# Strips of an image by half rows, turned on VectorE instead of TensorE

## The chip, the cores and the metric

The kernel runs on one core of a Trainium2 chip. The metric is the device time of one execution in microseconds (us); of several executions the median is taken. The engines are TensorE (PE, with its weight loads as PEld), VectorE (DVE), ScalarE (ACT), GpSimd (POOL) and SyncE (SP), which only issues DMAs here.

## The reference

The input x is 16 images of 56 x 56 pixels with 384 channels, fp32. Two layers follow one another, each added to its input:

```
x = x + window_attention(group_norm(x))      # 12 heads of 32, windows 7 x 7, image rolled by -3, -3
x = x + depthwise_3x3(group_norm(x))         # signs of the clipped weights
```

The group norm has 32 groups of 12 channels, over all pixels of an image. In the attention, q, k and v are products of the rolled image with a 1152 x 384 matrix; each window of 49 pixels attends to itself with a table of relative positions added, and masks for the windows that the roll has wrapped; a product with a 384 x 384 matrix and a bias follow, and the image is rolled back.

## The kernel before, in words

Channels lie on partitions, in three blocks of 128 (NC = 3). An image is cut into eight strips of seven rolled rows (NS = 8, 392 pixels, ST), numbered s through all images; a strip has two units of four windows (u). The units are the loop: `all_units` goes over 256 of them, and a unit has six slots. In each slot stands heavy work (`heavy`): value and query_key of the next strip, the projection of this one (py), the scores of the next unit. After the heavy work of slot 0 come the sums (L474), the attention products (po, L494), `invert` (ACT L512 and L513, DVE L514 and L515) and `divide` (DVE L522).

Everything else is light work. `at(when, f, ...)` gives it a time in units, and within a unit it is emitted behind the slot whose share of the unit it has reached. So the order of every engine is written out by this plan, and each engine works in that order. Two things are planned so: the second layer of the image before (`plan_conv`: eight taps of DVE for each of 12 bands, L621, and `store`), and the loading of the next image (`plan_load`).

Loading a strip before the change: `fetch` issues DMAs on SP's queue that bring whole pixels, 1536 bytes each, into one of two staging tiles (xl, pixels on partitions). `load` then, for each block c, has PE turn four pieces of 112 pixels into a PSUM bank (pl, L322), ACT copy the 392 columns into the strip's tile x in the order of windows (L325), and DVE take the statistics (bn_stats, L329). When the last strip is there, `norm_gather` and `norm_scale` make the image's coefficients by a chain of small DMAs and POOL operations. The first image's strips are loaded ahead of the loop in the same way. PSUM has four banks for pl, pq, pv, po, py and px in turn (`bank`), and the scores have the other four (ps). POOL's queue also has the copy and store of each strip's result (L553, L556) between the layers. The attention result `ot` comes from the pool `two`.

The last strip of an image wraps: it has four rows from the bottom and three from the top.

Of the kernel before, what the change touches and what calls it, by code (L numbers as in the profile page):

```python
# [9 lines left out]
F32 = mybir.dt.float32  # L10
# [5 lines left out]
WIN = 7  # L16
SHIFT = WIN // 2
# [17 lines left out]
def kernel(  # L35
# [12 lines left out]
    nc = tc.nc  # L48
    P = 128
    B, H, W, C = x.shape  # L50
    NH = rel_table.shape[1]
    D = C // NH
    NC = C // P
    HPC = P // D
    T = WIN * WIN
    NS = H // WIN
    NW = W // WIN
    ST = WIN * W
    UW = 4
    UPS = NW // UW  # L60
    NU = NS * UPS
# [2 lines left out]
    NB = H // BR  # L64
    R = W + SHIFT
    LT = 2 * W
    NL = -(-ST // LT)
    QT = HT + T
    OT = 2 * W
# [7 lines left out]
    const = ctx.enter_context(tc.tile_pool(name="const", bufs=1))  # L77
    dram = ctx.enter_context(tc.tile_pool(name="dram", bufs=3, space=bass.MemoryType.DRAM))
    xpool = ctx.enter_context(tc.tile_pool(name="x", bufs=11))
    io = ctx.enter_context(tc.tile_pool(name="io", bufs=3))  # L80
    two = ctx.enter_context(tc.tile_pool(name="two", bufs=2))
    vpool = ctx.enter_context(tc.tile_pool(name="v", bufs=2))
    ptpool = ctx.enter_context(tc.tile_pool(name="pt", bufs=3))
    bpool = ctx.enter_context(tc.tile_pool(name="xb", bufs=2))
# [2 lines left out]
    small = ctx.enter_context(tc.tile_pool(name="small", bufs=2))  # L87
# [3 lines left out]
    def bank(name):  # L91
        return ps.tile([P, 512], F32, tag="mm", name=name)
# [21 lines left out]
    vq = const.tile([P, 4, NW // 2, NC, D], F32, tag="vq", name="vq")  # L114

    xls = [const.tile([P, NL, C], F32, tag=f"xl{n}", name=f"xl{n}") for n in range(2)]

    es = const.tile([P, NH, 2, HT], F32, tag="e", name="e")

# [7 lines left out]
    def clear():  # L127
        for xl in xls:
            nc.gpsimd.memset(xl[:, NL - 1, :], 0.0)

        for t in spare:
            nc.gpsimd.memset(t[:, NL - 1, :], 0.0)

    def clear_more():
        nc.gpsimd.memset(power, -0.5)
        nc.gpsimd.memset(ones, 1.0)
        nc.gpsimd.memset(least, LEAST)
        nc.gpsimd.memset(seen, 0.0)
        for t in (qk[:, :, ST:], *hps):
            nc.gpsimd.memset(t, 0.0)  # L140

    def clear_again():
        for t in spare:
            nc.vector.memset(t, 0.0)
# [87 lines left out]
    stats, coefs, parts = {}, {}, {}  # L232
# [16 lines left out]
    def norm_scale(key, queue, pool=nc.gpsimd):  # L249

        gt = parts.pop(key)
        name = "%d_%d" % key
        g = small.tile([GROUPS, 4], F32, tag="g", name=f"g{name}")
        mean, var, rstd, shift = (g[:, n : n + 1] for n in range(4))
        if key[0]:
            var = seen[:GROUPS, key[1] : key[1] + 1]
        dev = small.tile([GROUPS, GS], F32, tag="dev", name=f"dev{name}")

        def fold(x):

            n = GS
            while n > 1:
                half = n // 2
                pool.tensor_tensor(x[:, :half], x[:, :half], x[:, n - half : n], ALU.add)
                n -= half

        pool.tensor_copy(dev, gt[:, :, 0])
        fold(dev)
        pool.tensor_scalar(mean, dev[:, 0:1], 1.0 / GS, None, ALU.mult)
        pool.tensor_tensor(dev, gt[:, :, 0], mean.to_broadcast([GROUPS, GS]), ALU.subtract)  # L270
        pool.tensor_tensor(dev, dev, dev, ALU.mult)
        pool.tensor_tensor(dev, dev, gt[:, :, 1], ALU.add)
        fold(dev)
        pool.tensor_scalar(var, dev[:, 0:1], 1.0 / GS, EPS, ALU.mult, ALU.add)
        nc.gpsimd.tensor_tensor(rstd, var, power[:GROUPS], ALU.pow)
        pool.tensor_tensor(shift, mean, rstd, ALU.mult)
        pool.tensor_scalar(shift, shift, -1.0, None, ALU.mult)
        both = small.tile([GROUPS, GS, 2], F32, tag="both", name=f"both{name}")
        pool.tensor_copy(both, g[:, 2:4].unsqueeze(1).to_broadcast([GROUPS, GS, 2]))
        by_channel = dram.tile([C, 2], F32, tag="cod", name=f"cod{name}")  # L280
        queue.dma_start(by_channel.rearrange("(g n) k -> g (n k)", n=GS), both.rearrange("g n k -> g (n k)"))
        coef = small.tile([P, NC, 2], F32, tag="coef", name=f"coef{name}", bufs=4)
        queue.dma_start(coef, by_channel.rearrange("(c p) k -> p c k", p=P))
        coefs[key] = coef
# [4 lines left out]
    xs = {}  # L289

    def staging(s):

        if NS > s >= 2 and s < 2 + len(spare) and staged:
            return spare[s - 2]
        return xls[s % 2]

    def fetch(s):
        b, r = divmod(s, NS)
        xl = staging(s)
        first = r * WIN + SHIFT  # L300
        for odd in range(2):
            t, end = 0, (WIN + 1 - odd) // 2
            while t < end:
                row = (first + odd + 2 * t) % H
                n = min(end - t, (H - row + 1) // 2)
                rows = x[b, row : row + 2 * n - 1 : 2].rearrange("t w c -> w t c")
                here = xl[odd * W : (odd + 1) * W, t : t + n, :]
                for lo, hi in ((SHIFT, SHIFT + 48), (SHIFT + 48, W), (W, R)):
                    nc.sync.dma_start(here[lo - SHIFT : hi - SHIFT], rows[lo % W : (hi - 1) % W + 1])
                t += n  # L310

    def load(s, c):
        b, r = divmod(s, NS)
        if (0, b) not in stats:
            stats[0, b] = small.tile([P, NC, NS, 6], F32, tag="st0", name=f"st0_{b}", bufs=1)
        if c == 0:
            xs[s] = xpool.tile([P, NC, ST], F32, tag="x", name=f"x_{s}")
        pt = bank(f"pl_{s}_{c}")
        for t in range(NL):

            n = min(LT, max(ST - t * LT, HT + 1))
            nc.tensor.transpose(  # L322
                pt[:, t * LT : t * LT + n], staging(s)[:n, t, c * P : (c + 1) * P], ident[:n, :n]
            )
        nc.scalar.copy(  # L325
            xs[s][:, c, :].rearrange("p (w r c) -> p r w c", r=WIN, c=WIN),
            pt[:, :ST].rearrange("p (r w c) -> p r w c", w=NW, c=WIN),
        )
        nc.vector.bn_stats(stats[0, b][:, c, r, :], xs[s][:, c, :])  # L329


# [310 lines left out]
    def at(when, f, *args):  # L642
        side.setdefault(int(when), []).append((when, f, args))
# [20 lines left out]
    def plan_load(b):  # L664

        for r in range(NS):
            when = NU * (b - 1) + max(1.3 + 1.2 * r, 2 * r - 3.9)
            if r < 2:

                at(max(NU * (b - 1) - 3 + 1.5 * r, 0.1 * r), fetch, b * NS + r)  # L670
            for c in range(NC):
                at(when + 0.9 * c / NC, load, b * NS + r, c)
            if r + 2 < NS:
                at(when + 0.7, fetch, b * NS + r + 2)
        at(when + 0.8, norm_gather, (0, b), nc.gpsimd)
        at(when + 0.9, norm_scale, (0, b), nc.gpsimd)

# [78 lines left out]
    with tc.manual_schedule():  # L756
        nc.scalar.preload_act_table_set("natural_log_exp_and_others")
        clear()
        staged.append(None)
        for s in range(2 + len(spare)):  # L760
            fetch(s)
        staged.clear()
        fetch_weights()
        clear_more()
        load_bias(nc.gpsimd, 0, 38, True)
        for s in range(NS):
            for c in range(NC):
                load(s, c)
            if s + 2 + len(spare) < NS:
                fetch(s + 2 + len(spare))  # L770
            if s % 2 and s > 1:
                load_weights(s // 2 - 1)
        norm_gather((0, 0), nc.sync)
        clear_again()
        norm_scale((0, 0), nc.sync, nc.vector)
        load_bias(nc.gpsimd, 38, T, True)
        load_weights(NC)
        load_depthwise()
        add_bias(True)
        normalize(0)  # L780
        all_units(True)


        worst = small.tile([P, 2], F32, tag="worst", name="worst")
        for n in range(2):
            nc.vector.tensor_scalar(reach[:, n], reach[:, n], MOST[n], None, ALU.is_lt)
        nc.vector.tensor_reduce(worst[:, 0:1], reach.rearrange("p n u -> p (n u)"), AX.X, ALU.min)
        fine = small.tile([P, B], F32, tag="fine", name="fine")
        nc.vector.tensor_scalar(fine, seen, 1.0e37, None, ALU.is_lt)
        nc.vector.tensor_reduce(worst[:, 1:2], fine, AX.X, ALU.min)  # L790
        pf = bank("pf")
        nc.tensor.matmul(pf[:, 0:2], ones, worst, start=True, stop=True)
        both = small.tile([P, 1], F32, tag="both_fine", name="both_fine")
        nc.vector.tensor_reduce(both, pf[:, 0:2], AX.X, ALU.add)
        nc.vector.tensor_scalar(again, both, -1.0, 2.0 * P, ALU.mult, ALU.add)
# [65 lines left out]
```

## Time and profile before

| | us |
|---|---|
| median of 3 runs (4452.28 to 4455.99) | 4454.59 |
| profiled execution, own time | 4451.33 |
| its span | 4449.5 |
| PE busy | 4267.8 (96%) |
| DVE busy | 3300.8 (74%) |
| ACT busy | 2372.4 (53%) |
| POOL busy | 488.8 (11%) |
| strip transposes, PE L322 (1488 from xl) | 199.1 |
| ACT copy out of PSUM, L325 | 198.9 |

In the profile's rows, "busy, mean ns" are the time of a group of like instructions and of one of them; behind the second bar stands the idle time of the engine ahead of them and what ended it. Busy times of PE overlap, because matmuls are pipelined: four transposes that show 0.56 us delay what follows by less. The 1.8 us between the span and the execution's own time lie around the span. In an answer by stretches, each row gives the length and the busy time of each engine within it; in an answer on waits, each row gives who waited for whom, the total, the number of times and the longest.

### The profile page before, as it was taken

Reading aid. Unit: us, or ns where it says so; the run is one execution under the profiler, and the core shown is the slowest. Engines: PE = TensorE matmul, PEld = TensorE weight load, DVE = VectorE, ACT = ScalarE, POOL = GpSimd, SP = SyncE. Lnnn points to the kernel's source line nnn. Section 1 sums busy time; section 2 is a strip of 40 time slices with the busy share of each in tenths; the row PEclk is TensorE's granted clock in tenths of the full one; section 3 lists DMA queues with packets and bytes.
Section 4 is the critical chain, followed back from the end, with each engine's and each line's share of the span. In section 5 each row is a group of like instructions: output and inputs, shape, how many; then the busy total and the mean of one; then the engine's idle time right before and its main releaser. Section 6 shows DMA issues by size and latency. Waiting matters only on the chain.

```text
span 4449.5 us, 156099 instructions
## 1 busy us (share of the span) xinstructions
PE 4267.8 (96%) x69481; PEld 2759.0 (62%) x69481; DVE 3300.8 (74%) x4267; ACT 2372.4 (53%) x4549; POOL 488.8 (11%) x1200
## 2 busy tenths in 40 slices
PE   5999999999999999999999999999999999999961
PEld 3666666666666666666666666666666666666641
DVE  3445777777777777777777777777777777777878
ACT  2445555555555555555555555555555555555542
POOL 3001110111102011010111101011110101111000
PEclk8999999999999999999999999999999999999985
DMA  3323444444444444344444444444444444433332
GB/s 89 72 64 84 96 99 117 96 103 105 103 94 109 109 94 112 91 99 115 93 107 108 99 96 106 111 97 105 99 102 107 96 110 103 108 94 86 95 89 88
DMA packets 987323, 439.24 MB, mean 99 GB/s; under 512 B 843490, under 2 KB 945387, under 8 KB 986642
## 3 DMA queue, kind: packets, MB, share of 16 engines
q1 hardware_dynamic: 960000, 344.92, 36.2%
q0 software_dynamic: 24464, 81.86, 5.2%
q8 instruction: 550, 9.01, 0.9%
q10 hardware_dynamic: 2178, 2.38, 0.2%
q14 instruction: 131, 1.07, 0.1%
HBM read 169.69 MB, written 158.47 MB: 74 GB/s over the span
## 4 chain that ended last, share of the span: by engine, by line
PE 94%; DVE 3%; DMA 1%; issue 1%; ACT 0%; SPq 0%; POOL 0%; ACTq 0%; DVEq 0%; POOLq 0%
PE pq L349 35%; PE pv L362 17%; PE py L533 17%; PE ps L403 7%; PE po L494 7%; PE ps L474 4%; PE pl L322 3%; PE px L632 3%; DVE o L621 2%; DMA xl<-in_x_dram 0%; SPq L385 0%; DMA out_dram<-xo 0%; DMA mvd<-mv 0%; DMA e<-in_x_dram 0%; DMA vq<-in_x_dram 0%
## 5 line engine op out<-in xcount | busy, mean ns | idle before, releaser
L349 PE MATMUL pq<-xn,wq_t 128*128 128x392 f32 x4608 | 1616.4, 498 | 2.2 <-issue 1.2
L621 DVE SCALAR_TENSOR_TENSOR o<-hp,dw_t,o 128x784 f32<-128x784 f32 x1536 | 1560.9, 1021 | 31.9 <-ACT o L608 17.7
L349 PEld LDWEIGHTS pq<-xn,wq_t 128*128 128x128 f32 x4608 | 837.1, 189 | 551.9 <-issue 6.6
L356 ACT COPY qk<-pq 128x392 f32<-128x392 f32 x768 | 373.3, 486 | 859.0 <-PE pq L349 858.3
L533 PE MATMUL py<-ot,wo_t 128*128 128x392 f32 x2304 | 819.7, 498 | 4.0 <-DVE ot L522 4.0
L362 PE MATMUL pv<-xn,wq_t 128*128 128x392 f32 x2304 | 821.1, 497 | 1.2 <-ACT xn L338 1.2
L514 DVE SCALAR_TENSOR_TENSOR ln<-ps,inv 128x588 f32<-128x588 f32 x256 | 197.3, 771 | 750.1 <-ACT inv L513 729.1
L533 PEld LDWEIGHTS py<-ot,wo_t 128*128 128x128 f32 x2304 | 420.3, 190 | 268.2 <-DVE ot L522 4.1
L362 PEld LDWEIGHTS pv<-xn,wq_t 128*128 128x128 f32 x2304 | 417.0, 189 | 270.8 <-ACT xn L338 2.4
L369 ACT COPY vt<-pv 128x392 f32<-128x392 f32 x384 | 190.1, 495 | 553.3 <-PE pv L362 553.2
L403 PEld LDWEIGHTS ps<-qk 32*64 32x64 f32 x24576 | 307.9, 131 | 149.2 <-issue 103.8
L438 ACT ACTIVATE e<-e 128x1176 f32<-128x1176 f32 x256 | 302.8, 1183 | 176.8 <-DVE e L420 176.8
L420 DVE SCALAR_TENSOR_TENSOR e<-ps,bias 128x1176 f32<-128x1176 f32 x256 | 350.2, 1368 | 38.8 <-PE ps L403 33.5
L494 PE MATMUL po<-e,v 49*32 49x49 f32 x24576 | 363.9, 212 | 12.4 <-DMA v<-vq 7.7
L494 PEld LDWEIGHTS po<-e,v 49*32 49x32 f32 x24576 | 355.4, 105 | 17.7 <-issue 13.4
L553 POOL COPY y<-y 128x63 f32<-128x63 f32 x128 | 32.1, 251 | 2915.8 <-DVE y L541 2915.8
L403 PE MATMUL ps<-qk 32*64 32x49 f32 x24576 | 341.6, 225 | 5.0 <-issue 4.5
L329 DVE BATCH_NORM_STATS2 st<-x 128x6 f32<-128x392 f32 x384 | 214.8, 561 | 135.1 <-ACT x L325 133.9
L632 PE MATMUL px<-ident,o 128*112 128x128 f32 x1344 | 202.6, 286 | 103.2 <-DVE o L621 89.2
L541 DVE TENSOR_TENSOR y<-py,x 128x392 f32<-128x392 f32 x384 | 215.8, 562 | 98.1 <-PE py L533 92.4
L325 ACT COPY x<-pl 128x392 f32<-128x392 f32 x384 | 198.9, 520 | 167.8 <-PE pl L322 167.8
L373 DVE STREAM_TRANSPOSE vq<-vt 128x512 f32<-128x512 f32 x384 | 269.0, 702 | 6.0 <-ACT vt L369 5.8
(114 smaller groups left out, 3486.5 us busy)
## 6 DMA issues: line engine op xcount, KB each, us to landing
v<-vq SPq DMA_DIRECT2D x2048, 48.0 KB
mid<-y POOLq DMA_DIRECT2D x112, 619.5 KB
out_dram<-xo SPq DMA_DIRECT2D x192, 336.0 KB
xb<-mid SPq DMA_DIRECT2D x96, 472.0 KB
xb<-mid SPq DMA_DIRECT2D x96, 442.5 KB
xl<-in_x_dram SPq DMA_DIRECT2D x108, 288.0 KB
xl<-in_x_dram SPq DMA_DIRECT2D x108, 216.0 KB
out_dram<-xo SPq DMA_DIRECT2D x64, 168.0 KB
```

What stands on the lines that cost most here:

```text
L349: nc.tensor.matmul(pq[:, :ST].rearrange("p (w t) -> p w t", t=T), wq_t[:, c, m * P : (m + 1) * P], xn[:, c, :, :T], start=(c == 0), stop=( ...
L356: nc.scalar.copy(qk[:, m, :ST], pq[:, :ST])
L362: nc.tensor.matmul(pv[:, :ST].rearrange("p (w t) -> p w t", t=T), wq_t[:, c, 2 * C + m * P : 2 * C + (m + 1) * P], xn[:, c, :, :T], start= ...
L373: nc.vector.transpose(vq[:, :, :, m].rearrange("p h n d -> p n h d"), vt[:, m].rearrange("p (n w) (j b) -> p n (w j) b", w=2, b=D),)
L403: nc.tensor.matmul(pp[row * HT : (row + 1) * HT, i, k0 : k0 + T], qk[part, NC * fast + j, q0 : q0 + HT], qk[part, NC * (not fast) + j, q0 ...
L420: nc.vector.scalar_tensor_tensor(e, pp[:, :, : NC * 2 * T].rearrange("q i (n k) -> q i n k", k=T), QSCALE, bias[:, int(s % NS == NS - 1)]. ...
L438: nc.scalar.activation(flat, flat, AF.Exp, accum_out=reach[:, 0, u : u + 1])
L494: nc.tensor.matmul(po[w][i * D : (i + 1) * D, (2 * j + r) * T : (2 * j + r + 1) * T], vs[s][keys, n * 2 + r, h * D : (h + 1) * D], by_head ...
L533: nc.tensor.matmul(py[:, :ST], wo_t[:, c, m * P : (m + 1) * P], ots[s][:, c, :], start=(c == 0), stop=(c == NC - 1),)
L541: nc.vector.tensor_tensor(view.rearrange("p r (w c) -> p w r c", c=WIN), py[:, :ST].rearrange("p (w r c) -> p w r c", r=WIN, c=WIN), xs[s] ...
L621: nc.vector.scalar_tensor_tensor(acc, hp[:, dy : dy + BR, dx : dx + W], dw_t[:, c, t : t + 1], acc, ALU.mult, ALU.add)
L632: nc.tensor.transpose(po[:OT, c * P : (c + 1) * P], flat[c][:, t * OT : (t + 1) * OT], ident)
```

## The change

Strips of the images 1 to 15 are brought in another form. `fetch_halves` takes one channel block of a strip and issues, on POOL's queue, one DMA for each 32 of its channels (four a block, 12 a strip; four times as many for the last strip of an image, which wraps). Each brings 15 half rows of 28 pixels; pixel t of a half row goes to partition t of the quarter, and a piece is 32 channels of one pixel, 128 bytes. Once all of a strip is there, `turn_halves` turns the whole tile in squares of 32 by one VectorE instruction, from xl into a new tile xt, so that channels lie on partitions. `arrange` then has ACT copy xt into the strip's tile x in the order of windows: two copies for the two halves of the rows, and a small one for the last three columns, which the roll takes from the other end; DVE's bn_stats follows as before. Nothing of the first image's loading changes, and `load` stays for it. The pool `two` has one buffer where it had two, which makes room for xt, and POOL clears both staging tiles between the first image's last strip and the loop.

```diff
-    two = ctx.enter_context(tc.tile_pool(name="two", bufs=2))
+    two = ctx.enter_context(tc.tile_pool(name="two", bufs=1))
...
+    xt = const.tile([P, NC, NR, D], F32, tag="xt", name="xt")
...
+    def halves(s):
+        flat = xls[s % 2].rearrange("p t c -> p (t c)")[:, : NC * NR * D]
+        return flat.rearrange("p (c k d) -> p c k d", c=NC, d=D)
+
+    def fetch_halves(s, c):
+        b, r = divmod(s, NS)
+        xz = halves(s)
+        flat = x[b].rearrange("h w c -> (h w) c")
+        first = r * WIN + SHIFT
+        rows = min(WIN, H - first)
+        cut = HR - SHIFT
+        for i in range(HPC):
+            def move(k, n, token, lo=0, hi=HR):
+                nc.gpsimd.dma_start(
+                    xz[i * D + lo : i * D + hi, c, k : k + n, :],
+                    flat[token : token + n * (hi - lo)].rearrange("(k t) c -> t k c", k=n)[
+                        :, :, c * P + i * D : c * P + (i + 1) * D
+                    ],
+                )
+            start = first * W + SHIFT - HR
+            if rows == WIN:
+                move(0, NR, start)
+                continue
+            n = 2 * rows
+            move(0, n, start)
+            move(n, 1, start + n * HR, 0, cut)
+            move(n, 1, 0, cut, HR)
+            move(n + 1, NR - n - 1, SHIFT)
+
+    def turn_halves(s):
+        nc.vector.transpose(
+            xt.rearrange("p c k d -> p (c k d)"), halves(s).rearrange("p c k d -> p (c k d)")
+        )
+
+    def arrange(s, c):
...
+        to = xs[s][:, c].rearrange("p (h w r c) -> p h r w c", h=2, r=WIN, c=WIN)
+        for h in range(2):
+            nc.scalar.copy(
+                to[:, h], xt[:, c, 1 + h : 1 + h + 2 * WIN - h : 2, :HR].rearrange("p r (w c) -> p r w c", c=WIN)
+            )
+        nc.scalar.copy(to[:, 1, :, NW // 2 - 1, WIN - SHIFT :], xt[:, c, 0 : 2 * WIN : 2, HR - SHIFT : HR])
         nc.vector.bn_stats(stats[0, b][:, c, r, :], xs[s][:, c, :])
...
             when = NU * (b - 1) + max(1.3 + 1.2 * r, 2 * r - 3.9)
+            s = b * NS + r
             if r < 2:
-                at(max(NU * (b - 1) - 3 + 1.5 * r, 0.1 * r), fetch, b * NS + r)
+                for c in range(NC):
+                    at(max(NU * (b - 1) - 3 + 1.5 * r + 0.3 * c, 0.1 * r), fetch_halves, s, c)
+            at(when, turn_halves, s)
             for c in range(NC):
-                at(when + 0.9 * c / NC, load, b * NS + r, c)
-            if r + 2 < NS:
-                at(when + 0.7, fetch, b * NS + r + 2)
+                at(when + 0.2 + 0.2 * c, arrange, s, c)
+                if r + 2 < NS:
+                    at(when + 0.7 + 0.3 * c, fetch_halves, s + 2, c)
...
         clear_again()
+        for xl in xls:
+            nc.gpsimd.memset(xl, 0.0)
```

HR is 28 (half a row), NR is 15, D is 32 and HPC is 4.

More of the change, by code (lines that the diff above doesn't have):

```diff
@@ L66 @@
     LT = 2 * W
+    HR = W // 2
+    NR = 2 * WIN + 1
     NL = -(-ST // LT)
@@ L328, in load @@
         )
+        nc.vector.bn_stats(stats[0, b][:, c, r, :], xs[s][:, c, :])
+    def halves(s):
[30 more added lines that the diff above has]
+    def arrange(s, c):
+        b, r = divmod(s, NS)
+        if (0, b) not in stats:
+            stats[0, b] = small.tile([P, NC, NS, 6], F32, tag="st0", name=f"st0_{b}", bufs=1)
+        if c == 0:
+            xs[s] = xpool.tile([P, NC, ST], F32, tag="x", name=f"x_{s}")
+        to = xs[s][:, c].rearrange("p (h w r c) -> p h r w c", h=2, r=WIN, c=WIN)
[4 more added lines that the diff above has]
+        nc.scalar.copy(to[:, 1, :, NW // 2 - 1, WIN - SHIFT :], xt[:, c, 0 : 2 * WIN : 2, HR - SHIFT : HR])
         nc.vector.bn_stats(stats[0, b][:, c, r, :], xs[s][:, c, :])
```

## The prediction

> **What bounds the kernel now.** I read the page's first two parts, then the chain that ended last, then the stretches of one image, then the order of time around single strips.
>
> ```profile
> PE 4267.8 (96%) x69481; PEld 2759.0 (62%) x69481; DVE 3300.8 (74%) x4267; ACT 2372.4 (53%) x4549; POOL 488.8 (11%) x1200
> ...
> PE   5999999999999999999999999999999999999961
> PEclk8999999999999999999999999999999999999985
> ```
>
> PE is busy 9 tenths or more from the second slice to the 38th, at the full clock. The chain, asked for 340 to 3941 us, is PE alone; the strips' transposes (pl, L322) hold 3.7% of it:
>
> ```profile
> by line: PE pq L349 36.7%; PE pv L362 18.3%; PE py L533 18.2%; PE ps L403 7.7%; PE po L494 7.3%; PE ps L474 4.0%; PE pl L322 3.7%; PE px L632 3.5%; issue 0.3%; DMA out_dram<-xo 0.1%; ACT xn L338 0.1%; ACT xo L633 0.0%; ACT e L438 0.0%; ACT
> ```
>
> One image is 16 units. Cut at the unit starts of the eighth image (columns: stretch, length, busy PE, PEld, DVE, ACT, POOL, clock, DMA share), units 1 to 10 hold all eight strip loads of the next image, 11 to 15 none:
>
> ```profile
> 1959.79:2127.37 167.58, 167.58 (x2740) 109.05 (x2739) 130.27 (x171) 93.97 (x182) 13.71 (x36) 1.00 0.45 104
> 2127.37:2208.12 80.75, 80.75 (x1340) 51.69 (x1340) 60.77 (x74) 45.33 (x86) 12.12 (x30) 1.00 0.47 107
> ```
>
> PE has no idle there; DVE has 37.3 us of 167.6, and the waits say where it goes:
>
> ```profile
> DVE ln L514 <- ACT inv L513: 26.8, 10, 5.2
> DVE st L329 <- ACT x L325: 5.9, 5, 2.0
> ```
>
> Once a unit DVE stands waiting for ACT's reciprocal (2.7 us on average): it has caught up with PE. That wait is DVE's reserve.
>
> **What the Trainium skill says.** "VectorE: DVE Perf Modes", section The three transpose paths: VectorE turns only blocks of 32 by 32, each for itself. The trace has this instruction (L373, row below). "DMA: Bandwidth & Descriptors", section Specifications: under 512 bytes a piece a transfer is below line rate. The trace agrees: q1's 786,432 packets of 128 bytes (SBUF to SBUF) take 13.3 ns each, 9.6 bytes a ns; its packets of 1536 bytes 96 ns, 15.9 bytes a ns. The same page, section SWDGE vs HWDGE vs iDMA: a DMA issued from GpSimd has its descriptors computed in software there, gathered into packets of preferably at most 4096 bytes. The trace agrees on the gathering: a coef load of 384 pieces of 8 bytes shows as 16 packets. "SBUF — State Buffer", section Who interferes with whom: a VectorE instruction with two SBUF inputs contends with GpSimd instructions that read SBUF. The trace shows nothing of it for DMA issues: L621 takes 1015 ns beside a POOL DMA issue (167 cases), 1021 ns with POOL idle.
>
> **Part 1: transposes leave PE.** 15 images x 8 strips x 3 channel blocks = 360 groups of four. What a group costs is not its busy time but how far it pushes the next matmul:
>
> ```profile
> 2111.57 1.27 PE L494 MATMUL po<-e,v 49*32 49x49 f32 x96
> 2112.77 0.56 PE L322 MATMUL pl<-ident,xl 112*128 112x112 f32 x4
> 2113.17 0.55 PE L362 MATMUL pv<-xn,wq_t 128*128 128x392 f32 x1
> ...
> 2127.90 1.26 PE L494 MATMUL po<-e,v 49*32 49x49 f32 x96
> 2129.09 0.60 PE L349 MATMUL pq<-xn,wq_t 128*128 128x392 f32 x1
> ```
>
> With a group: 2112.77 to 2113.17, 0.40 us. Without one, the next matmul starts where the group did (1.19 us after po against 1.20). Counted over the trace, 150 groups behind po or ps cost 0.404 us and 210 behind large matmuls 0.350: 60.6 + 73.5 = **134 us off PE**. (3.7% of the chain would make 145; I take the start-to-start sum.) They also leave 360 uses of the four PSUM banks, a relief I count as nothing.
>
> **Part 2: DVE gets a turn a strip.**
>
> ```profile
> L373 DVE STREAM_TRANSPOSE vq<-vt 128x512 f32<-128x512 f32 x384 | 269.0, 702 | 6.0 <-ACT vt L369 5.8 <-issue 0.2
> L513 ACT ACTIVATE inv<-ln 128x588 f32<-128x588 f32 x256 | 177.5, 693 | 8.1
> L438 ACT ACTIVATE e<-e 128x1176 f32<-128x1176 f32 x256 | 302.8, 1183 | 176.8 <-DVE e L420 176.8
> L325 ACT COPY x<-pl 128x392 f32<-128x392 f32 x384 | 198.9, 520 | 167.8 <-PE pl L322 167.8
> ```
>
> The turn moves 3 x 15 x 32 = 1440 elements a partition. In proportion to L373 that is 1.97 us; with L373's time as one element a cycle of 0.96 GHz (533 ns) plus 169 fixed it is 1.67. I take 1.67, x120 = **200 us of DVE**. It waits for 12 landings or more, whose waits I put at 0.25 us (bounds 0 and 0.5; a wait instruction on DVE shows 21 ns). In units 1 to 10: 130.3 + 8 x 1.92 = 145.6 us in 167.6 - 24 x 0.373 = 158.6 us, 92%. Idle left: 13 us, where L514 and st now wait 32.7. It fits only if DVE runs 1.9 us a unit later behind PE.
>
> **Part 3: ACT.** One copy of 392 out of PSUM (520 ns) becomes two of 196 and one of 21 out of SBUF. From L513 and L438: (1183 - 693)/588 = 0.83 ns an element, 203 fixed. So 2 x 366 + 220 = 0.95 us, +0.43 a block, **+156 us**, 58% of the shorter span; if these patterns cost twice the slope, +270. Beside PE's work. New waits: ACT waits for the turn, and queued behind it are the qk and vt copies that free PSUM banks for PE and feed the scores. The arrange is put at least one of a unit's six slots (2.8 us) behind the turn, so ACT waits only where DVE is over 1.1 us late. Then bn_stats waits for ACT as it does now, 0.43 us longer.
>
> **Part 4: the loads go from SP to POOL.** Some six SP issues a strip become 12 POOL DMAs (48 for an image's last strip): 132 an image. The nearest row, 384 pieces each:
>
> ```profile
> L283 POOL DMA_DIRECT2D coef<-cod x30: 800/802/807, 288.5 to 4087.1; - x30
> ```
>
> At 0.8 us, about 100 us an image, 37% of POOL's time, against 11% now. A strip takes 9.6 us to issue where strips follow at 1.2 units (19 us). Behind it on POOL: the norm chains (units 0 and 10.9 of an image, no fetch between -0.9 and 2.0 or after 8.6), the y copies and mid stores, delayed by at most four issues, 3.2 us, whose readers come units later. Landing: that coef load has landed 2.4 us after its issue begins. One fetch is 420 pieces of 128 bytes; at 13 ns and 30 pieces an engine 0.4 us of DMA. The last quarter is issued 1.1 units (17 us) before its turn. A strip adds 12 x 0.4 x 14/16 = 4.2 us an engine where the old pieces took 392 x 96/16 = 2.4 us; in these units the DMA share goes from 0.45 to about 0.55. Price 0; bounds: the HBM read of 128 bytes isn't in the trace; at three times 13 ns it still fits (12.6 of 19 us). SP's relief: 0 to 3 us.
>
> **Part 5: ot with one buffer, the clearing.** The ACT copy into ot follows matmuls that stand behind the last readers (py) in PE's order; price 0. The two memsets on POOL (1536 elements each; a memset of 928 takes 0.86 us on POOL, so 2.9 for both) fall in POOL's 21 us wait for DVE's variance; price 0, at most 2.9.
>
> **What comes late next.** In odd units, PE's py waits for DVE's division (L522), which ends 0.8 to 2.1 us ahead of it on average over the images. Five of eight strips lose one or two PE groups just there, 0.35 to 0.75 us, while ACT, which sets L514's start, has 0.43 us a block more and sometimes waits for a turn. The exponential ends 2.7 to 4.7 us ahead of its readers. So a lag of 1.9 us is mostly but not wholly carried. I let a fifth of the turn through, 0.34 us a strip x 120 = 41 us. Bounds: 0; and 0.67 us, 80.
>
> **Sum.** Against the profiled execution: 4451.3 - 134 + 41 = 4358. The median of the runs is 3.3 us above it: **4361 us**.
>
> **Rivals.** *All is hidden:* 4454.6 - 134 = 4320. For it: L514's 2.7 us waits. Against: the 0.8 us ahead of py. *DVE becomes the bound in units 1 to 10 (slower):* turn, its waits and the three longer arranges pass to PE in full, 1.92 + 1.3 = 3.2 us a strip, less 1.12 saved, x 120 = +250: 4705. It decides from 1.12 us of stall a strip on, that is if two thirds of a turn get through. For it: 92% and in-order waits; against: DVE catches up each unit, and in units 11 to 15 has 25% left. *The pieces land late:* the point is 1.6 us a DMA (19/12). At 2 us, 8 x 24 - 159 = 33 us an image, +500. Against: 0.8 to issue, 2.4 to land. *Nothing moves:* stalls match 134 us. That transposes stay is excluded: the plan calls load no more for images 1 to 15.
>
> **How the numbers follow.** 0.2% (9 us) is about what a measurement tells from no change. All hidden or nearly (under 4335) 0.22; partly hidden, to 4400, 0.48; to 4440, 0.15: faster 0.85. Within 9 us: 0.03. DVE bound 0.08 and late pieces 0.04: slower 0.12. The range 4316 to 4440 leaves some 0.03 below and 0.15 above.
>
> **What would show it.** L322 at 96 matmuls, PE near 4135 us busy; a turn at 1.6 to 2.0 us; L514's wait halved; PE waits for DVE ot (py) or ACT of some tens of us; POOL near 48%. It is wrong if DVE waits for x's landing in most turns, if POOL's issue exceeds 1.5 us, or if PE idles over 134 us in the middle.

## The result, and the profile after

The changed kernel takes 4298.76 us (median of 4, 4297.24 to 4300.28) against 4455.29 for the one before: ratio 0.9649, 95% interval 0.9632 to 0.9666, 156.5 us less. The forecast was 4361, range 4316 to 4440: right in direction, and too slow by 62 us. The profiled executions differ by 152.6 us (4451.33 and 4298.77); the traces below account for these.

First the engines' row of the page after, then the chain for 330 to 3800 us:

```profile
PE 4125.1 (96%) x68041; PEld 2628.4 (61%) x68041; DVE 3478.0 (81%) x4387; ACT 2479.2 (58%) x5269; POOL 1800.4 (42%) x3182
```

```profile
by line: PE pq L404 38.2%; PE pv L417 19.0%; PE py L588 18.8%; PE ps L458 7.9%; PE po L549 7.5%; PE ps L529 4.1%; PE px L687 3.7%; issue 0.1%; DMA xb<-mid 0.1%; DVE e L475 0.1%; DMA out_dram<-xo 0.1%; DVE o L676 0.1%; DVE xt L368 0.0%; ACT 
```

The chain is PE as before, without pl; the turn (xt) holds 0.0% of it, and no strip load shows. The same stretches of the eighth image, units 1 to 10 and 11 to 15 (length, then busy PE, PEld, DVE, ACT, POOL, clock, DMA share, GB/s):

```profile
1886.22:2044.77 158.55, 158.55 (x2650) 100.60 (x2658) 140.02 (x175) 101.21 (x230) 84.44 (x144) 1.00 0.50 110
2044.77:2125.52 80.75, 80.75 (x1347) 51.60 (x1355) 62.76 (x79) 45.29 (x86) 29.65 (x55) 1.00 0.52 111
```

Units 1 to 10 went from 167.58 to 158.55 us, where the forecast's sum without stalls had 158.6. DVE is at 88%, and PE still has no idle time. Units 11 to 15 have not changed. The new instructions, and DVE's wait for their data:

```profile
L368 DVE STREAM_TRANSPOSE xt<-xl 128x1440 f32<-128x1440 f32 x120 | 200.4, 1670 | 0.4 <-DMA xl<-in_x_dram 0.4
L380 ACT COPY x<-xt 128x196 f32<-128x196 f32 x720 | 225.8, 369 | 93.8 <-DVE xt L368 92.6
L383 ACT COPY x<-xt 128x21 f32<-128x21 f32 x360 | 76.5, 212 | 11.4
L351 POOL DMA_DIRECT2D xl<-in_x_dram x1980 | 1328.8, 724 | 179.7 <-DVE xt L368 105.1 <-issue 29.0 <-DMA mid<-y 24.9
```

A turn takes 1.67 us; of 120 turns one waited for a load, 0.4 us. And DVE's reserve over the whole execution, before, after, and after in units 1 to 10 of the eighth image:

```profile
DVE ln L514 <- ACT inv L513: 729.1, 247, 8.4
```

```profile
DVE ln L569 <- ACT inv L568: 536.5, 236, 8.4
```

```profile
DVE ln L569 <- ACT inv L568: 14.6, 9, 2.6
```

It is 193 us less, but not all of that went to the 200 us of turns: the units are shorter too, and the run without the turn below parts the two. In units 1 to 10 of the second to the fifteenth image this wait fell from 2.7 us to 1.5 on average, and in 15 of these 140 units nothing was left of it.

### The profile page after: what moved, and what is told of

The parts are those of the page before. It is cut to its first block, busy times and chain, and to the rows that moved or that the text cites. A ratio compares the mean times of both kernels' runs of the same rounds, so it can differ in the third digit from the quotient of the medians.

```text
span 4297.0 us, 155602 instructions
## 1 busy us (share of the span) xinstructions
PE 4125.1 (96%) x68041; PEld 2628.4 (61%) x68041; DVE 3478.0 (81%) x4387; ACT 2479.2 (58%) x5269; POOL 1800.4 (42%) x3182
## 4 chain that ended last, share of the span: by engine, by line
PE 94%; DVE 3%; DMA 1%; issue 1%; ACT 0%; SPq 0%; POOL 0%; ACTq 0%; DVEq 0%; POOLq 0%
PE pq L404 36%; PE pv L417 18%; PE py L588 18%; PE ps L458 7%; PE po L549 7%; PE ps L529 4%; PE px L687 3%; DVE o L676 2%; SPq L440 0%; DMA xl<-in_x_dram 0%; DMA wl<-in_L_conv_w_out_dram 0%; DMA xn<-in_x_dram 0%; DMA out_dram<-xo 0%; DMA vq<-in_x_dram 0%; DMA e<-in_x_dram 0%
## 5 line engine op out<-in xcount | busy, mean ns | idle before, releaser
L404 PE MATMUL pq<-xn,wq_t 128*128 128x392 f32 x4608 | 1591.4, 497 | 0.0
L351 POOL DMA_DIRECT2D xl<-in_x_dram x1980 | 1328.8, 724 | 179.7 <-DVE xt L368 105.1
L569 DVE SCALAR_TENSOR_TENSOR ln<-ps,inv 128x588 f32<-128x588 f32 x256 | 197.0, 769 | 540.2 <-ACT inv L568 536.5
L380 ACT COPY x<-xt 128x196 f32<-128x196 f32 x720 | 225.8, 369 | 93.8 <-DVE xt L368 92.6
L688 ACT COPY xo<-px 112x384 f32<-112x384 f32 x448 | 195.1, 482 | 123.7 <-PE px L687 94.1
```

The source lines that it names most:

```text
L351: nc.gpsimd.dma_start(xz[i * D + lo : i * D + hi, c, k : k + n, :], flat[token : token + n * (hi - lo)].rearrange("(k t) c -> t k c", k=n) ...
L404: nc.tensor.matmul(pq[:, :ST].rearrange("p (w t) -> p w t", t=T), wq_t[:, c, m * P : (m + 1) * P], xn[:, c, :, :T], start=(c == 0), stop=( ...
```

## The experiments

Twelve kernels ran, each beside the kernel before on the same chip (medians 4451.9, 4452.6 and 4454.5 us in the three batches). The kernel after was not run again in them, so a difference to its 4298.76 us can be off by the some 3 us by which these medians differ.

**The price of PE's groups.** On the kernel after, in `plan_load`:

```diff
             for c in range(NC):
+                at(when + 0.9 * c / NC, groups, s, c)   # bank(), then four transposes of ident
                 at(when + 0.2 + 0.2 * c, arrange, s, c)
```

> The kernel after, with the 360 groups of four transposes put back on PE at their old times, of a constant (the identity) into a PSUM bank that nobody reads; loads, turn and arrange stay as changed. Theory A (a group costs 0.35 to 0.40 us on PE, 138 us in all with the slower second matmul behind it, and the rest of the 156 us came from somewhere else than PE's own work): 4437 us, 138 above the kernel after. Theory B (all 156 us are the groups' own price, 0.43 us each): 4455 us, back at the kernel before.

Measured: 4430.35 us, ratio to before 0.9955 (0.9941 to 0.9968). The groups cost 131.6 us by the medians, or 136 by the two ratios to before: as theory A has it, and within 3 us of the forecast's count. But with all of PE's old work back, the kernel is still 21.6 us faster than the one before. Theory B falls. In the traces, 224 units from the second image on (from the first attention product of a unit to that of the next) take 3711.0 us before and 3693.5 here, with the same number of matmuls.

Where these 17.5 us were, PE's waits of the kernel before tell (340 to 4218 us; total, times, longest):

```profile
PE po L494 <- issue: 4.0, 3, 1.6
PE ps L403 <- issue: 3.5, 9, 0.6
PE pq L349 <- issue: 1.2, 2, 0.8
```

"issue" means that PE waited for nothing the profile shows. One of them, in unit 11 of the seventh image, in order of time:

```profile
1860.11 1.22 PE L494 MATMUL po<-e,v 49*32 49x49 f32 x91
1862.88 0.32 PE L494 MATMUL po<-e,v 49*32 49x49 f32 x5 [1.55 <-issue]
```

PE stops in the midst of 96 matmuls whose inputs all lie there, and takes up the last five after 1.55 us of idle time. In the trace's instruction queue (q8, 550 packets of 16 KB for the 140,266 instructions that PE has in the trace, so some 256 in a packet) a packet begins 0.14 us ahead of the stop, counted from the start of the last matmul ahead of it, and ends 1.92 us after it, 2.06 us long where the median is 1.1. Of the ten packets that begin within 4.5 us behind the store of unit 11 (below), nine last 1.7 to 3.1 us. For the stops in the scores the sign is another one: the packets beside those of the list last 0.9 to 1.4 us, but all ten of over 0.25 us from start to start fall on the same place of PE's instructions counted modulo 256 (193 or 194), wherever in its unit that place lies. So the traces are read here as PE running out of instructions: 96 small matmuls and their loads are used up in 1.3 us, and the next packet was late. The longest stop is followed by six matmuls at down to half speed, 1.7 us more together.

**What makes the packets late.** Five edits of the kernel before. Without the strips' DMAs:

```diff
-                at(max(NU * (b - 1) - 3 + 1.5 * r, 0.1 * r), fetch, b * NS + r)
+                pass
...
-            if r + 2 < NS:
-                at(when + 0.7, fetch, b * NS + r + 2)
```

> The kernel before, without the strips' DMAs of images 1 to 15 (their strips are left as they lie in the staging tiles, so x of these images is not loaded; everything else runs). Theory A (the strips' DMAs on SP's queue held up PE's instruction supply: some 18 stalls without a releaser, 13 to 15 us, in units 2, 8 and 11 of an image): 4441 us, the stalls gone. Theory B (the stalls belong to PE's own instruction stream and are not due to these DMAs): 4455 us, the stalls still there.

Measured: 4441.56, ratio 0.9977 (0.9969 to 0.9985), 10.4 us less. PE's waits in the same stretch:

```profile
PE po L494 <- issue: 6.7, 7, 1.5
PE pq L349 <- issue: 0.6, 1, 0.6
```

The stops in the scores, which were in units 2, 4 and 8, are gone from the list; those of unit 11, in the attention and just behind it, stay. Theory A is half right.

In unit 11 it is the next image's norm that begins: POOL stores the statistics to DRAM (mvd, 384 pieces of 8 bytes), 0.8 us ahead of the unit. Planned later:

```diff
-        at(when + 0.8, norm_gather, (0, b), nc.gpsimd)
-        at(when + 0.9, norm_scale, (0, b), nc.gpsimd)
+        at(when + 0.95, norm_gather, (0, b), nc.gpsimd)
+        at(when + 1.0, norm_scale, (0, b), nc.gpsimd)
```

> The kernel before, with the norm of the next image (norm_gather and norm_scale of the strips) planned 0.15 and 0.1 units later, in unit 11 behind the attention instead of at the end of unit 10. Theory A (in the kernel before, the small store of the statistics, issued 0.8 us ahead of unit 11, slows the fetch of PE's next block of instructions just when the attention's short matmuls use it up): the stalls in unit 11 go, some 8 us faster than the kernel before. Theory B (these stalls are due to the place in PE's instruction stream alone): no change, the stalls stay in unit 11.

Measured: 4445.58, 0.9987 (0.9979 to 0.9995), 7 us less. The stops in the attention are gone, but stops in unit 11 are not: they moved from 1.55 to 9.6 us into it, 3.6 us behind the store's new place (5.93), where the next scores are. They follow the store, not a place in the program. The same with the strips' DMAs gone:

> The kernel before, without the strips' DMAs of images 1 to 15 (their strips are not loaded, as in the run without strip DMAs) and with the norm planned later. Theory A (two disturbances of PE's instruction supply add up): all stalls without a releaser go, 18 to 20 us off the kernel before, 4432 us, the time of the changed kernel with its groups put back. Theory B: as the run without strip DMAs, 4441 us.

Measured: 4439.89, 0.997 (0.9959 to 0.9981), not the 4432 of theory A, since the later store only hits other matmuls: unit 11 keeps 4.9 us in its trace (table below). So the store was left out instead:

```diff
+        if key[0] == 0 and key[1] > 0:
+            by_channel = first_channels[0]     # image 0's
+        else:
...
             by_channel = dram.tile([C, 2], F32, ...)
             queue.dma_start(by_channel.rearrange("(c p) k -> p c k", p=P), mv)
...
```

> The kernel before, without the store of the first statistics of images 1 to 15 to DRAM (their coefficients are made from image 0's). Theory A: the stalls of unit 11 go, those of units 2 and 8 stay, 8 to 10 us below the kernel before. Rival: no change.

Measured: 4439.80, 0.9966 (0.9952 to 0.9979), 14.7 us less, more than the 8 to 10 expected. What stays are the scores alone:

```profile
PE ps L410 <- issue: 3.7, 8, 0.8
```

> The kernel before, without the strips' DMAs of images 1 to 15 and without the store of these images' first statistics to DRAM (the coefficients of the first layer are made from image 0's; strips are not loaded). Theory A (PE's instruction supply is disturbed by two things, the strips' DMAs and the small store ahead of unit 11): all stalls without a releaser go, 4432 us, some 20 us below the kernel before, the time of the changed kernel with its groups put back. Rival (the store isn't it): 4441 us, as without the strips' DMAs alone, stalls still in unit 11.

Measured: 4433.87, 0.9953 (0.994 to 0.9967), 20.7 us less. In its list of PE's waits for that stretch there is no line at all, as in that of the kernel with the groups put back. Theory A, in its second form, holds: two disturbances, 10 and 15 us by themselves, 21 together, where the intervals are 4 to 6 us wide to each side. The time of all 224 units in the traces shows which disturbance sits where, in us above this run, by the unit of the image:

| kernel before | unit 2 | 8 | 14 | 11 | all |
|---|---|---|---|---|---|
| as it is | 3.9 | 2.0 | 3.1 | 8.9 | 17.8 |
| no strips' DMAs | 0.1 | 0.1 | -0.2 | 11.2 | 11.9 |
| store later | 3.6 | 0.9 | 2.9 | 4.4 | 14.4 |
| no strips' DMAs, store later | 0.0 | 0.3 | -0.3 | 4.9 | 5.5 |
| no store | 4.7 | 1.1 | 3.0 | 0.1 | 9.4 |

The strips' DMAs cost in units 2, 8 and 14, the store in unit 11. Each row is one execution; that without strips' DMAs was its kernel's second slowest of 14, so its sum is above what the medians say. A rival would be the PSUM banks: in the run with the groups put back, no copy of ACT holds the banks of pl any more. The traces answer it: this run has all the old copies out of these banks, and its 224 units take 3693.2 us, against 3693.5 there.

In the kernel after one line is left (340 to 4070 us):

```profile
PE ps L458 <- issue: 0.8, 2, 0.5
```

The strips no longer come by SP. Their gathered packets from POOL hardly stopped PE here, but they are no proof against it: in the trace of the kernel after without its turn (next part), the slowest of five executions, three stops, 3.5 us together, stand in the scores of unit 4, at the same place modulo 256 (193).

```profile
PE ps L458 <- issue: 3.5, 3, 1.5
```

The store is issued 1.46 us into unit 11 and not 0.8 us ahead of it, as the attention's burst ends. With the groups put back it is issued 0.36 us into it, and without the turn at its start; neither trace has a stop in unit 11. So in all three kernels, whose strips come by POOL, a store 0.8 to 2.2 us later than before goes with no stop in unit 11. That this shift is the cause was not tried by moving the store back alone.

**What the turn costs.** On the kernel after, without the turn:

```diff
-            at(when, turn_halves, s)
...
+        nc.vector.memset(xt, 1.0)
```

> The kernel after without any turn (the tile that the turn writes is filled once, so the strips of images 1 to 15 hold a constant; loads, arranges and everything else run, but nothing on the engines waits for the loads). Theory A (the turn and its wait for the loads cost nothing on the path): within 5 us of the kernel after. The forecast's term: some 20 to 40 us faster than the kernel after.

Measured: 4297.34 (0.9656, 0.9643 to 0.9669), 1.4 us below the kernel after by the medians and 3 above it by the ratios: the turn costs nothing that can be told from zero. What it uses up on DVE shows beside the kernel after, first without the turn, then with it:

```profile
DVE ln L569 <- ACT inv L568: 624.4, 253, 8.4
DVE st L384 <- ACT x L383: 120.4, 92, 3.4
```

```profile
DVE st L384 <- ACT x L383: 41.8, 45, 2.1
```

88 us of the turns' 200 come out of the wait for the reciprocal (624.4 to 536.5) and 79 out of the statistics' wait for ACT. The other 105 us that the reserve lost against before (729.1 to 624.4) are not the turn's. With a second one right behind it (the call to `nc.vector.transpose` twice):

> The kernel after, with each strip's turn issued twice in a row (the second repeats the first): DVE has 1.67 us a strip more, 200 us in all. Theory A (DVE's wait for ACT's reciprocal, 536 us in the kernel after, is a reserve that takes up added DVE work): within 10 us of the kernel after, that wait down to some 380 us. The forecast's term (a fifth of a turn gets through to PE): 40 us or more slower than the kernel after.

Measured: 4337.78 (0.9748, 0.9734 to 0.9761), 39 us slower. That is the forecast's fifth, but for the second turn, not the first. DVE's reserve fell as theory A said, yet PE waits now:

```profile
DVE ln L572 <- ACT inv L571: 412.1, 172, 8.4
ACT x L383 <- DVE xt L371: 263.4, 101, 4.3
PE pv L420 <- DVE y L599: 22.4, 27, 1.2
PEld pv L420 <- ACT e L496: 22.5, 13, 1.8
```

412 us of reserve are left and are of no use, for they lie elsewhere: in units 1 to 10 0.66 us a unit are left, and none in 69 of 140 units. ACT stands up to 4.3 us for the turns, with the copies that PE needs behind it. The same second turn, half a unit away:

```diff
             at(when, turn_halves, s)
+            at(when + 0.65, turn_halves, s)
```

> The kernel after, with a second turn of each strip that stands half a unit behind the first (behind the three arranges) instead of back to back. DVE's total is that of the run with the turn twice. If DVE's total load sets the cost: 4338 us as there. If it is the length of one block of DVE work ahead of the copies and sums that wait for it: within 15 us of the kernel after, 4315 us or less.

Measured: 4303.82 (0.9661, 0.9648 to 0.9674), 5 us slower than the kernel after, with the same DVE work as the run before:

```profile
DVE ln L569 <- ACT inv L568: 403.3, 145, 8.4
ACT x L380 <- DVE xt L368: 126.7, 86, 3.6
```

The reserve is as low (0.59 us a unit in units 1 to 10, none in 96 of 140 units), DVE is busy 94% of these units in both runs, ACT's wait is half. It is how the DVE work is placed that costs, not DVE's total. The two runs don't tell whether it is the length of the one block or that the second turn stood ahead of ACT's copies there and behind them here. Three in a row:

> The kernel after, with each strip's turn issued three times in a row, 400 us more of DVE. The first turn cost nothing and the second 39 us; if the reserve ran out with the second, the third passes in full for a part of the strips: 4338 + 100 us or more. If a constant fifth passes: 4378 us.

Measured: 4521.5 in a single execution, 223 us above the kernel after: no constant share. The first turn cost nothing, the second 39 us, the third 184.

**POOL's queue.** In `fetch_halves`:

```diff
-                nc.gpsimd.dma_start(
+                nc.sync.dma_start(
```

> The kernel after, with the half rows' DMAs issued on SP's queue instead of POOL's. The forecast held POOL's queue to cost nothing and the pieces to land in time; on SP, 12 DMAs a strip stand among 16 of v, each holding the queue for about 0.8 us, 22 us of the 19 to 33 us a strip has. If SP's queue becomes late: v comes late for the attention, PE waits for it, 50 us or more slower than the kernel after. If the queue doesn't matter: within 10 us of it.

Measured: 4419.77 (0.9929, 0.9913 to 0.9944), 121 us slower than the kernel after. PE's waits:

```profile
PE po L549 <- DMA v<-vq: 72.5, 30, 6.5
```

On SP the same pieces make v late, and 62 large matmuls between 340 and 4000 us stand some 0.65 us apart instead of 0.33, as behind the long stop above, 20 us in all. The queue is a condition of the gain. An issue of the pieces held SP for 0.445 us (median, up to 2.8), not for the 0.8 expected. The DMA engines are not busier (SP's and POOL's queues take 45.4% of their time, 45.1 in the kernel after), so what makes v late is not the amount of transfer. Whether it is the order of issue on SP or that each piece is a packet of its own there was not parted. On POOL's queue, a packet gathers 30 pieces, 3840 bytes, and takes 290 ns, 9.7 ns a piece.

**A further step that failed.** On the kernel after, the results too are turned on DVE and stored in pieces:

```diff
+    def store_squares(b, k, c):
...
+        nc.vector.transpose(z.rearrange("p k d -> p (k d)"), o.rearrange("p k d -> p (k d)"))
...
+        for i in range(HPC):
+            nc.gpsimd.dma_start(rows[:, :, c * P + i * D : c * P + (i + 1) * D], z[i * D : i * D + HR])
```

> A further step on the kernel after: the results of images 0 to 14 are turned by DVE in squares of 32 too (taps work on half rows padded to 32, one turn of 896 elements a band and block, 1.1 us), and stored by POOL in pieces of 128 bytes; PE's transposes px (some 135 us of PE) and ACT's copies behind them go. DVE gets 200 us more, as in the run with two turns, where that cost 39 us. If it only adds up: 4298.8 - 135 + 40 = 4204 us. If the added DVE work finds no reserve, or small stores to DRAM come late or slow PE's instruction supply: 4250 us or more; no gain from 4299 on.

Measured: 4314.22 (0.969, 0.9676 to 0.9705), 15 us slower than the kernel after. Its output is not the reference's, for a reason that stays open, so the time stands for the work alone. Its chain, and PE's waits:

```profile
PE 48%; DVE 15%; POOL 12%; DMA 10%; SPq 8%; issue 6%; ACT 2%; DVEq 0%; ACTq 0%; POOLq 0%
```

```profile
PE po L549 <- DMA v<-vq: 51.2, 63, 5.4
PE py L588 <- DVE ot L577: 33.1, 24, 3.9
```

PE has 79 us less work than after and loses them again, on v and on DVE's division: the bound is shared by PE, DVE and the DMAs. This step does not beat the kernel after.

## Why the prediction was wrong, by its steps

- **Part 1, 134 us off PE:** 131.6 measured (136 by the ratios). Right.
- **Part 2, the turn:** 1.67 us, as forecast. With both sizes measured its form can be worked out: 702 ns for 512 elements and 1670 for 1440 are 1.04 ns an element (0.96 elements a ns) and 0.17 us fixed. The 0.25 us a turn for landings was nothing.
- **Part 3, ACT:** 369 and 212 ns where 366 and 220 were worked out. ACT's busy time rose by 107 us, not 156, since copies that follow one another overlap: 720 of 369 ns make 266 us and are busy for 225.8.
- **Part 4, POOL and the loads:** 0.72 us an issue (0.8 forecast), POOL at 42% (48%), DMA share 0.50 in units 1 to 10 (0.55), one late load. Price 0 was right. What it priced at 0 to 3 us as "SP's relief" was the first wrong term: 392 whole pixels a strip leaving SP's queue freed PE from stops in units 2, 8 and 14, 10 us on its own. The list of before already showed such stops; the sum had no term for them.
- **Part 5:** no wait of it shows in PE's chain.
- **What comes late next, 41 us:** the second wrong term, and the larger. "I let a fifth of the turn through": the first turn lets nothing through (1.4 us). The reserve was read rightly, 2.7 us a unit; the error was to charge a part while one turn (1.67) and its waits still lay under it. DVE at 92% of a stretch was taken for a sign of stalls. It reached 88%, and even 94% cost only 5 us when the second turn stood apart. PE's wait for the division, where the fifth was to pass, is 3.9 us in the whole execution, and was 4.0 before.
- **The range:** its low end, 4316, was the case "all is hidden" at 4320. That case took PE for gapless but for the groups. The waits listed under "issue" were left out of the sum, though the list of before had them, 8.7 us in three lines. The units' lengths make it 17.8, since the list leaves out part of each delay: in the scores it has 3.5 us where the starts of neighbouring matmuls show 6.4.

Together: 131.6 and the stops of the traces (17.5 us in 224 units, 18.7 scaled to 15 images) make 150 of the profiled 152.6 us. Of the rivals, the one that all is hidden was nearest; a turn that passes to PE nearly in full came only with the third (184 of 200 us), and in the kernel after one of 120 turns waited for a piece.

## What to carry to other kernels

When a busy engine sheds work, ask of the work that another engine takes on not only what share of it that engine is busy, but how long one block of it is, and who waits behind it with what slack; split or move the block before giving up. Count the stops that the profile gives to nothing ("issue"): on an engine that uses short instructions in bursts they can be its instruction supply, and other DMAs gave or took some 20 us there in this kernel. And try the queue: the same transfer was worth 121 us more on a queue that v does not use.

## What the runs showed of the hardware that was not expected

- PE's instructions come in packets of 16 KB. A store of 3 KB to DRAM in pieces of 8 bytes was followed by packets of up to 3.1 us (3.4 in the run without strips' DMAs; median 1.1) and by stops of PE of up to 1.6 us; without it, 14.7 us less for 15 stores. How the store holds up the fetch stays open.
- Reading DRAM in pieces of 128 bytes was no slower than moving them within SBUF: 9.7 ns a piece in POOL's gathered packets, against 13.3 for SP's single ones before. With the strips' pieces on SP too, one packet each, the mean of all 128-byte pieces was 13.1.
